# Layer 0 of a four-layer network: six instead of seven of eight half tiles convolved on TensorE, and other preferences in the schedule

## The chip, the cores and the metric

The kernel runs on one core of a Trainium2 chip. The metric is the device time of one execution in microseconds (us). Three runs of the kernel before gave 6812.61, 6817.96 and 6801.19 us, so the median is 6812.61 us. The engines are called by the profile's names: PE is TensorE (matmuls), PEld its weight loads, DVE VectorE, ACT ScalarE, POOL GpSimd, and SP the queue that issues most DMAs.

## The reference, cut to what matters

The input is a batch of 16 images with 96 channels of 56 x 56 pixels. Four layers follow each other. The change touches layer 0, a masked, channel-selected inverted bottleneck with a 3 x 3 depthwise convolution:

```python
logits = _conv1x1(x, w_mask) + b_mask[None, :, None, None]
mask = (logits >= 0).astype(x.dtype)
...
s = jax.nn.sigmoid(pooled @ w_sal.T + b_sal)
k = int(round(BUDGET * HID))
thr = lax.top_k(s, k)[0][:, -1:]
vector = (s >= thr).astype(x.dtype)
h = jax.nn.relu(_bn(_conv1x1(x, w_pw1), bn1_g, bn1_b, bn1_m, bn1_v)) * mask_dilate
h = h * vector[:, :, None, None]
h = jax.nn.relu(_bn(_dwconv3x3(h, w_dw), bnd_g, bnd_b, bnd_m, bnd_v)) * mask
h = h * vector[:, :, None, None]
h = _bn(_conv1x1(h, w_pw2), bn2_g, bn2_b, bn2_m, bn2_v) * mask
return x + h
```

Of 576 hidden channels each image keeps the 288 with the largest saliency. Layer 1 is a state-space block with scans, layers 2 and 3 are Fourier mixing with a quantized MLP. They stay as they are.

## The kernel before, in words

The four layers run one after the other: `layer0`, `layer1` and `layers23` each fill the core, and an image goes from one to the next through DRAM. A second version of layer 0 (`layer0_all`) stands behind a condition for inputs with a tie among the selected channels; it isn't executed here.

**Tiles of layer 0.** The 288 kept channels of an image are gathered into two full groups of 128 (group 0 and group 1) and a rest of 32. An image is cut into two halves of 28 rows. A half tile is 128 channels by 28 x 56 = 1568 pixels. For each image and group there are two half tiles; the rests of two images and both their halves are packed into one further tile, the mixed one (`MIX`). A pair of images therefore has nine tiles, the eight half tiles and the mixed one, and there are eight pairs. Among them are 32 half tiles of group 0.

**The path of a half tile** (`worker`). POOL clears the border row of a padded buffer (L797). PE multiplies the image by the chosen rows of the first weight (L816, tile `p`), ACT applies the batch norm and the relu and writes the padded buffer `pad` (L820). Then the 3 x 3 depthwise convolution follows, in one of two ways:

- On VectorE: one multiplication for the first tap (L863) and eight fused multiply-adds for the others (L865), each over the whole tile, 128 x 1568. ACT then applies norm and relu in place (L868).
- On TensorE: for each of two halves of the tile, nine taps times four 64 x 64 quarters of products with a diagonal weight, 36 products into the PSUM tile `p_c` (L838), from which ACT takes norm and relu in three pieces (L855).

`on_pe` decides which way it is: only tiles of group 0 go to TensorE, and of these all first halves, the second halves of even images, and those of images with b % 4 == 3. These are 28 of 32, or seven of eight. Group 1 and the mixed tile go to VectorE. VectorE thus has 32 + 4 half tiles and 8 mixed tiles.

**The choice of channels** (`vectors`), once for each image, ahead of its tiles: the image is loaded (L691) into one of four buffers `x`; ACT sums it (L695); VectorE makes the mean (L697, L699); PE forms the saliencies (`p_s`, L705); VectorE and ACT compare and count (L713, L720, L725, L726, L735, L737), with PE between them (`p_n`, L729 and L731); PE gathers the selected weights (`p_w` L744, `p_r` L752 and L758); ACT and VectorE copy them out (L747, L763, L770, L771, L775).

**The end of a half image** (`ends`), in two pieces: six products add up the three tiles (L887, L890), ACT takes the batch norm (L896), two products form the mask (`p_m`, L902), VectorE applies it and adds the image (L904, L907), and SP writes the result (L909). After the last piece the image buffer is free, and the next load may start.

**What sets the order.** Each of these steps is announced as an `Op` with an engine and an estimated cost. `in_order` keeps for every engine the time up to which it is planned, and again and again picks the step with the smallest sum of its possible start and a lead from a table (by engine and generator: `('DVE', 'ends')` is VectorE's part in `ends`); a negative lead lets a step go ahead of others. The pick is then emitted. So the table and the costs fix the order in which every engine executes, at the time of building; on the chip each engine takes its queue in that order and waits by semaphores. Buffers are planned too: four PSUM pairs `ps`, four images `x`, four padded buffers `pad`, twelve results `h`, two `y` and one `out`.

Of the kernel before, what the change touches and what calls it, by code (L numbers as in the profile page):

```python
# [59 lines left out]
def packed(x):  # L60
# [96 lines left out]
    for m in (C, DIN):  # L157
# [58 lines left out]
 'layer0': {'buffers': {'ps': 4, 'x': 4, 'pad': 4, 'h': 12, 'y': 2, 'out': 1},  # L216
            'leads': {('PE', 'worker'): 0.9,
                      ('DVE', 'worker'): 1.1,
                      ('DVE', 'ends'): 0.8,
                      ('ACT', 'vectors'): 0.1,  # L220
                      ('PE', 'filled'): 0.5,
                      ('ACT', 'ends'): -1.2,
                      ('ACT', 'filled'): -0.7,
                      ('SP', 'ends'): -0.2,
                      ('PE', 'vectors'): -0.1}},
 'layers23': {'buffers': {'ps': 4,
                          'xn': 2,
                          'xt': 1,
# [389 lines left out]
def layer0(ctx, tc, src, dst, flags):  # L618
# [49 lines left out]
        return Op("ACT", over + n * each, **k)  # L668

    def on_pe(b, g, half):  # L670
        return g == 0 and (b % 2 == 0 or half == 0 or b % 4 == 3)

    MIX = 2
    tiles = []
# [108 lines left out]
    def worker():  # L783
        while tiles:
# [40 lines left out]
            yield [filled(*run) for run in RUNS]  # L825
            h = hs[tile_] = buf([P, HALF * S], "h")
            if half != MIX and on_pe(b, g, half):
                taps, turn = its[0]["taps"][g], its[0]["turned"][g]
                for c in range(0, 4, 2):
# [1174 lines left out]
```

## Time and profile before

| | |
|---|---|
| median of three runs | 6812.61 us |
| the profiled execution | 6803.33 us |
| its span | 6801.4 us |
| PE, PEld, DVE, ACT, POOL busy over the span | 87%, 59%, 78%, 68%, 25% |
| mean granted clock of PE | 0.918 |
| layer 0 ends at | 1072 us |
| a VectorE tap (L865), 288 on half tiles | 1845 ns |
| the PE convolution (L838), 4032 records | 344.8 us busy |

The profile is one execution. Rows of groups give the line, the engine, the operation, output and input with shapes, the count, busy time and the mean of one in ns, and behind the last bar the engine's idle time just before and what ended it. A TensorE product of 32-bit numbers leaves two matmul records, so the 28 tiles of 72 products leave 4032. The records of one engine overlap a little; from start to start is the pace. Rows of waits give the waiting instruction, the one waited for, the total in us, the number and the longest. Rows in order of time begin with the start and the duration in us.

### The profile page before, as it was taken

The page shows a single profiled execution, that of the slowest core. Times are in us where ns is not written, and L with a number is a line of the kernel's source. Part 1 is how long each engine was busy: PE and PEld are TensorE (multiplying, and loading weights), DVE is VectorE, ACT ScalarE, POOL GpSimd, SP SyncE. Part 2 cuts the span into 40 slices and gives each one's busy share as a digit, 9 for nine tenths or more (in the row PEclk, how much of TensorE's full clock was granted, in tenths as well). Part 3 has the DMA queues.
Part 4 walks back from the last instruction along what each step waited for, and adds up shares of the span by engine and source line. Part 5 has one row for each costly group of instructions (what it writes and reads, how often), then busy time and mean ns, then how long its engine had stood idle before and what let it go on. Part 6 is the DMA issues. An engine that isn't in the chain of part 4 may idle for free.

```text
span 6801.4 us, 113297 instructions
## 1 busy us (share of the span) xinstructions
PE 5940.8 (87%) x45643; PEld 4042.6 (59%) x45643; DVE 5310.6 (78%) x6829; ACT 4627.4 (68%) x5959; POOL 1712.4 (25%) x1137
## 2 busy tenths in 40 slices
PE   7999997788888888888888776798999999999985
PEld 4455443244544455555555444687888888888875
DVE  6988892688888888888887893676787887878774
ACT  5555553788888888888888772466666666666664
POOL 0000001244444444444443442111111111111110
PEclk9999997788989888988889877899999999999997
DMA  1111111554444444444544441555555555555552
GB/s 41 42 40 36 40 29 51 147 149 139 141 135 142 137 135 142 134 143 141 145 132 126 125 133 53 118 116 125 129 121 127 120 125 134 138 137 121 123 112 64
DMA packets 508375, 763.72 MB, mean 112 GB/s; under 512 B 206337, under 2 KB 339137, under 8 KB 504530
## 3 DMA queue, kind: packets, MB, share of 16 engines
q1 hardware_dynamic: 506818, 753.53, 42.6%
q8 instruction: 362, 5.93, 0.4%
q0 software_dynamic: 1024, 2.85, 0.1%
q14 instruction: 171, 1.40, 0.1%
HBM read 563.65 MB, written 192.59 MB: 111 GB/s over the span
## 4 chain that ended last, share of the span: by engine, by line
PE 40%; DVE 33%; ACT 13%; issue 6%; DMA 5%; POOL 3%; SPq 1%; DVEq 0%; ACTq 0%; POOLq 0%
DVE h L865 4%; DVE dt L1345 4%; PE p_g L1511 3%; PE p_c L1209 3%; PE p_c L838 3%; DVE drive L1353 3%; DVE a L1359 2%; PE p_f L1501 2%; PE p_v L1803 2%; PE p_u L1821 2%; PE p_d L1276 2%; PE p L1756 2%; DVE hc L1325 2%; ACT big L1230 2%; PE p L1857 2%
## 5 line engine op out<-in xcount | busy, mean ns | idle before, releaser
L1382 POOL TENSOR_TENSOR big<-big,hc 128x784 f32<-128x784 f32 x384 | 776.5, 2022 | 1240.8 <-DVE hc L1325 1199.2
L1698 POOL TENSOR_TENSOR r<-v,nhalf 112x12 f32<-112x12 f32 (+1 forms) x128 | 357.0, 2798 | 2149.4 <-DVE v L1696 1263.1
L1345 DVE TENSOR_TENSOR dt<-dt,big 128x784 f32<-128x784 f32 x384 | 517.8, 1348 | 195.0 <-ACT a L1292 193.6
L865 DVE SCALAR_TENSOR_TENSOR h<-pad,rows,h 128x1568 f32<-128x1568 f32 x288 | 526.5, 1845 | 4.4
L1283 ACT ACTIVATE dt<-p_d,l_dtb 128x784 f32<-128x784 f32 x384 | 350.2, 912 | 176.0 <-PE p_d L1276 150.0
L1501 PE MATMUL p_f<-zt,w_fc 96*128 96x448 f32 x672 | 374.9, 704 | 85.2 <-ACT zt L1494 68.6
L1756 PE MATMUL p<-k_f,z 112*128 112x112 f32 x3072 | 392.1, 289 | 61.6 <-DVE h L1728 28.2
L1276 PE MATMUL p_d<-proj,l_dt 32*128 32x392 f32 x1536 | 391.0, 592 | 61.0 <-ACT hid L1503 36.3
L1353 DVE TENSOR_TENSOR drive<-dt,bc 128x784 f32<-128x784 f32 x384 | 430.3, 1121 | 9.3
L1209 PE MATMUL p_c<-x,taps 64*64 64x392 f32 x4608 | 425.5, 500 | 11.7 <-ACT big L1230 9.0
L1756 PEld LDWEIGHTS p<-k_f,z 112*128 112x128 f32 x3072 | 381.7, 205 | 72.5 <-issue 33.5
L1511 PE MATMUL p_g<-l_fc,hid 128*112 128x96 f32 x2688 | 393.7, 290 | 0.9 <-ACT hid L1503 0.9
L1325 DVE TENSOR_TENSOR hc<-a,bc 128x784 f32<-128x784 f32 x384 | 379.6, 989 | 3.1 <-POOL big L1382 3.1
L1285 ACT ACTIVATE dt<-dt,one 128x784 f32<-128x784 f32 x384 | 363.8, 947 | 9.3
L1511 PEld LDWEIGHTS p_g<-l_fc,hid 128*112 128x112 f32 x2688 | 358.2, 207 | 18.3 <-issue 10.7
L1734 PE MATMUL p<-h,k_f 112*128 112x192 f32 x1792 | 338.1, 337 | 31.7 <-DVE h L1728 17.3
L1292 ACT ACTIVATE a<-dt,aneg 128x784 f32<-128x784 f32 x384 | 348.1, 938 | 4.9 <-DVE a L1359 3.0
L1361 DVE TENSOR_TENSOR_SCAN a<-a,drive 128x784 f32<-128x784 f32 x192 | 350.2, 1824 | 0.5
L1359 DVE TENSOR_TENSOR_SCAN a<-a,drive 128x784 f32<-128x784 f32 x192 | 350.2, 1824 | 0.0
L1725 PE MATMUL p_a<-first,xt 97*112 97x192 f32 x1792 | 325.5, 333 | 27.4 <-ACT xt L1719 18.7
L838 PE MATMUL p_c<-pad,taps 64*64 64x392 f32 x4032 | 344.8, 491 | 0.1
L1725 PEld LDWEIGHTS p_a<-first,xt 97*112 97x112 f32 x1792 | 292.0, 180 | 55.1 <-ACT xt L1719 20.2
(339 smaller groups left out, 14268.0 us busy)
## 6 DMA issues: line engine op xcount, KB each, us to landing
bc<-bc SPq DMA_DIRECT2D x256, 784.0 KB
bc<-bc SPq DMA_DIRECT2D x256, 392.0 KB
d<-y SPq DMA_DIRECT2D x448, 192.0 KB
z<-d SPq DMA_DIRECT2D x128, 672.0 KB
d<-uu SPq DMA_DIRECT2D x256, 169.8 KB
z<-d SPq DMA_DIRECT2D x192, 194.0 KB
xc<-x SPq DMA_DIRECT2D x96, 336.0 KB
x<-in_x SPq DMA_DIRECT2D x16, 1176.0 KB
```

The source lines that it names most:

```text
L838: nc.tensor.matmul(p[to : to + 64, t, :TC], taps[64 * s : 64 * s + 64, i], pad[64 * s : 64 * s + 64, r0 : r0 + 7, i % 3 : i % 3 + S], star ...
L865: nc.vector.scalar_tensor_tensor(out, view, taps9[:, i : i + 1], out, ALU.mult, ALU.add)
L1209: nc.tensor.matmul(p[to : to + 64, b, :TC], taps[64 * s : 64 * s + 64, j, k], pad[64 * s : 64 * s + 64, r0 : r0 + 7, k % 3 : k % 3 + S], s ...
L1276: nc.tensor.matmul(p[:, b, :TC], wdt[on, i], proj[on, h], start=True, stop=True)
L1325: nc.vector.tensor_tensor(hc, a, t[:, 1], ALU.mult)
L1345: nc.vector.tensor_tensor(as_own(dt), as_own(dt), own(u), ALU.mult)
L1353: nc.vector.tensor_tensor(b, dt, t[:, 0], ALU.mult)
L1382: nc.gpsimd.tensor_tensor(out, out, hc, ALU.add)
L1501: nc.tensor.matmul(p[:, 0, :T], w_fc1[:, P * j : P * j + P], zt, start=True, stop=True)
L1511: nc.tensor.matmul(p[:Q, q, :C], hid[:, j, own], fc2[:, j], start=j == 0, stop=False)
L1725: nc.tensor.matmul(p[:Q, j, :HW], xt[:, at + j], w["first"], start=True, stop=True)
L1756: nc.tensor.matmul(p[:, q, :Q], flat[:, P * (3 * q + k) : P * (3 * q + k) + P], f2, start=True, stop=True)
```

## The change

The second halves of images 3, 7, 11 and 15 no longer fall to TensorE in `on_pe`, so that six of eight half tiles of group 0 stay there and VectorE convolves the others. The table of leads for layer 0 is another: some entries have other values (VectorE and SP in `ends` and PE in `vectors` change sign), the one of ACT in `filled` is gone, and those of POOL in `worker` and PE in `ends` are new. The numbers of buffers stay.

```diff
             'leads': {('PE', 'worker'): 0.9,
                       ('DVE', 'worker'): 1.1,
-                      ('DVE', 'ends'): 0.8,
+                      ('DVE', 'ends'): -0.2,
                       ('ACT', 'vectors'): 0.1,
                       ('PE', 'filled'): 0.5,
                       ('ACT', 'ends'): -1.2,
-                      ('ACT', 'filled'): -0.7,
-                      ('SP', 'ends'): -0.2,
-                      ('PE', 'vectors'): -0.1}},
+                      ('SP', 'ends'): 0.4,
+                      ('POOL', 'worker'): -2.6,
+                      ('PE', 'vectors'): 0.4,
+                      ('PE', 'ends'): -0.1}},
...
     def on_pe(b, g, half):
-        return g == 0 and (b % 2 == 0 or half == 0 or b % 4 == 3)
+        return g == 0 and (b % 2 == 0 or half == 0)
```

The changed program is one line longer ahead of these functions, so its lines from L226 on have a number higher by one: L838 becomes L839.

## The prediction

> **What bounds the kernel now.** The change lies in layer 0 alone; behind it the two programs issue the same instructions in the same order on all five engines. So I read layer 0 first: where it ends, then who is busy in it, then who waits in it. The stretches (us, busy time of PE, PEld, DVE, ACT, POOL, granted clock, DMA share, GB/s) say:
>
> ```profile
> 0.00:54.00 54.00, 18.64 (x91) 12.22 (x95) 14.46 (x56) 15.59 (x24) 13.09 (x24) 1.00 0.46 110
> 54.00:1072.00 1018.00, 1001.58 (x6692) 507.94 (x6684) 884.56 (x975) 551.22 (x735) 16.62 (x76) 1.00 0.13 34
> 1040.00:1072.00 32.00, 27.59 (x133) 13.13 (x123) 10.10 (x12) 7.60 (x8) 0.00 (x0) 0.99 0.16 48
> 1072.00:6801.00 5729.00, 4920.59 (x38868) 3522.43 (x38868) 4411.61 (x5798) 4060.58 (x5201) 1682.66 (x1037) 0.90 0.49 126
> ```
>
> Layer 0 ends at 1072: the next layer's first VectorE instruction waits there for the last output DMA. From the first VectorE convolution (54) on, PE is busy 98% of the time at full clock, VectorE 87%. Next, the groups that the change touches, and the waits of PE (54 to 1072) and of VectorE (54 to 1040, where its last convolution ends):
>
> ```profile
> L865 DVE SCALAR_TENSOR_TENSOR h<-pad,rows,h 128x1568 f32<-128x1568 f32 x288 | 526.5, 1845 | 4.4
> L838 PE MATMUL p_c<-pad,taps 64*64 64x392 f32 x4032 | 344.8, 491 | 0.1
> L863 DVE TENSOR_SCALAR h<-pad,rows 128x1568 f32<-128x1568 f32 x36 | 37.0, 1029 | 16.3 <-ACT pad L820 16.2
> ...
> PE p_s L705 <- DVE wide L699: 5.0, 3, 2.5
> PE p_n L729 <- DVE chosen L726: 2.9, 4, 2.3
> ...
> DVE y L904 <- PE p_m L902: 29.2, 9, 5.9
> DVE rest L770 <- ACT rows L763: 23.1, 6, 6.1
> DVE h L863 <- ACT pad L820: 16.2, 6, 4.6
> ```
>
> PE's waits come to 13 us in all, VectorE's (seven rows) to 104. So PE sets the pace and VectorE waits for what PE feeds it. Last, one turn of the image buffers, in order of time:
>
> ```profile
> 581.21 1.48 PE L902 MATMUL p_m<-x,l_mask 96*96 96x392 f32 x4
> 584.51 1.03 DVE L904 SCALAR_TENSOR_TENSOR y<-p_m,nmask,y 96x784 f32<-96x784 f32 x1
> 585.57 0.97 DVE L907 TENSOR_TENSOR out<-y,x 96x784 f32<-96x784 f32 x1
> 586.98 0.37 SPq L691 DMA_DIRECT2D x<-in_x  x1
> 594.62 2.82 ACT L695 ACTIVATE x<-x 96x3136 f32<-96x3136 f32 x1 [3.18 <-DMA x<-in_x]
> 597.56 0.15 DVE L697 TENSOR_SCALAR mean<-mean 96x1 f32<-96x1 f32 x1 [0.76 <-ACT x L695]
> 598.18 1.21 PE L705 MATMUL p_s<-l_sal,wide 97*128 97x288 f32 x4 [2.54 <-DVE wide L699]
> ```
>
> Image b+4 is loaded into the buffer that image b leaves: from the end of the last mask product of one (582.7) to the first product of the other (598.2) take 15.5 us, and PE waited 2.5 of them.
>
> **The change, part by part.**
>
> *Removed from PE.* on_pe loses the second half of images 3, 7, 11 and 15: 4 of 28 half tiles. Each costs 344.8/28 = 12.3 us of PE, together 49.3. Their six ACT evictions each (L855, (75.4+37.8)/28 = 4.0 us) give way to one L868 of 1.7: ACT loses 9 us and is busy 54% anyway, so I count nothing.
>
> *Added to VectorE.* Four times one L863 and eight L865. Busy time of such a tile is (526.5+37.0)/36 = 15.65 us, so 62.6 in all. It needs cover: 104 us of waits.
>
> *The order.* The other preferences change what stands behind what. In the old order 116 of 352 taps follow a tap of the same convolution, in the new one 26 of 384; elsewhere two convolutions alternate. The trace prices this: four taps in a row from 1022.89 to the next instruction at 1030.32, 1.86 each; alternating ones at 93.22, 94.99 and 96.75, 1.77 each. Ninety fewer pairs at 0.09 give 8 us back. So VectorE gets 54 us net. Output DMAs and image loads keep their number and sizes; the SP queue gains no entry in layer 0. The POOL queue keeps its pad memsets in number (80 and 0.2 us each), only in another order of pads.
>
> *PE alone.* Its last large product ended at 1067.2; less 49.3 gives 1018. From there to the layer's end is 4.9 as before (VectorE mask and add, then the last DMA): 1023.
>
> *VectorE alone.* From its first tap at 54: 48 tiles at 8 x 1.77 + 1.04 = 15.2 (730), 60 of the 64 output units at 1.03 + 0.97 = 2.0 (120; four stand behind the last tap), 15 selections of 6.1 (92: five L713, five L737, the small copies and L775), and the 9 us that it waits before 85, where the programs are still alike. The last tap ends at 1005. Behind it come L868 and a signal (1.9), then the products of the last image's half that still need it (fifteen in the order from the second on, 0.66 each: 9.9), then 4.9: 1022.
>
> Both queues alone thus reach about 1022, 50 below 1072. That is the limit of the gain. What is lost by their waiting for each other:
>
> (a) *The end.* In the new order the second mask product of image 12's second half has 92.7 us of PE work behind it (each product at its pitch in the trace: 0.66 us for 392 columns, 0.75 and 0.47 for the fills of 448 and 280, 6.1 for half a p_c tile), so PE reaches it at 1018 - 92.7 = 925. VectorE's L904 for it has 95 us of VectorE work behind it up to the last tap. So this tap can't end before 1020, and the layer not before 1020 + 16.7 = 1037. Loss 14. Late here is the last image: PE stands idle some 12 us before its last ten us of products.
>
> (b) *Image turns.* For images 4 to 14, even ones, the new order leaves 14.2 us of PE work between the two ends of the chain of the fourth block; it took 15.5 there. That is 1.3 for each of six images, 8 us; the old order had shorter distances twice (13.0 and 13.7 us), worth about 4. VectorE waits in the same turns, ahead of taps queued behind L697, but these are covered as PE is late by as much. Ends: 0 to 12; I take 4.
>
> (c) *The cold clock.* The row of 1040 to 1072 grants 0.99 to the last products, with no long gap ahead of them; by it (a)'s last 9.9 us cost 9.9. Against that speaks the Trainium skill, "TensorE: Matmul & The Clock Gate", section "What's actually happening": an array idle for one window of some 3.4 us is gated to half its clock, and comes back after some 3.4 us of activity. The change makes just such a gap. The trace agrees in kind: after PE's 10.3 us of idling at the layer's end the clock granted from 1075 to 1100 is 0.50. Half clock for 3.4 us adds 1.7, for all ten 9.9; I take 2, since the products are dense.
>
> (d) *The first 250 us.* VectorE is behind there, and products that reuse a PSUM buffer stand up to 6 us ahead of the L904 that frees it, as they already did. I take 2, ends 0 to 8.
>
> Sum: -50 + 14 + 4 + 2 + 2 = **-28 us**, the layer ends at 1044. Against the profiled execution (6803.33 us; span 6801.4, 1.9 around it) this gives 6775. The median of the runs shown is 6812.61, 9 above that execution; the forecast for the median is 6812.6 - 28 = **6784**.
>
> One reading has to be defended. The Trainium skill, "Perfetto Trace Analysis", section "Identifying the Most-Contended Engine", calls matmul busy time a bad measure and wants weight-load time instead. By that PE is loaded to 508/1018 = 50%, VectorE at 87% is the most contended, and 54 us more on it are a loss of up to 54. I hold with the waits: a busy row could hide slack, but an engine with slack would wait, and PE waits for others 13 us in 1018. A half tile's 36 products always take about 6.1 us, so they have no room to give.
>
> **The rivals.** *Clean gain*: image turns and end cost little more than (a) at its smallest, since VectorE's 54 us fit into 104 us of waits; about -43, 6770. Against it: the three ends above are in the order itself. *Half of it*: stalls chain, because both queues are full and only four pads and four PSUM pairs lie between them; each pair of images loses 2 to 3 us more, 8 x 2.5 = 20: -8, 6805. For it: old VectorE waits reach 6 us each. *VectorE becomes the bound, slower*: the place is L904 and L770, whose releasers (PE's mask product, ACT's copy of the rows) are fed late by VectorE itself. Its 104 us of waits would have to stay while its work grows: the last tap would end at 996 + 104 = 1100 and the layer at 1117, +45, 6857; taking half of the added work as lost, +20, 6833. It decides from the point where VectorE still waits over 59 us between first and last tap (1072 - 16.7 - 996). Against it: these waits are PE's pace, and PE is shortened. *That the change doesn't do what it says* can be excluded: the new program has 24 half tiles in L838's successor and 384 taps.
>
> **How the numbers follow.** Likeliest (-18 to -40) 0.64; clean (-40 to -50) 0.10; half (-18 to 0) 0.16; slower 0.10. A measurement of this kernel tells about 0.3% (20 us) from no change. Faster takes all of clean and 0.58 of the likeliest: 0.68. Same takes the remaining 0.06 and the half case: 0.22. Slower by over 20 us: 0.10, all of the third rival. The range leaves out that rival and the very best: 6765 to 6805; the likeliest alone is 6773 to 6795.
>
> **What would show it.** Right: L839 x3456 with about 296 us, L866 x320 with rows and x64 with the mixed tile, mostly 1.77 apart, layer 0's end (VectorE's wait for the last DMA) near 1044, VectorE over 95% busy from 54 to 1020, its waits there under 40 us, PE's waits up from 13 to about 30, one of them near the end of some 12 us. Everything after layer 0 unchanged in length. Wrong: VectorE's waits at 60 us or more, PE waits for L904 or L699 spread over all pairs, a clock under 0.95 inside layer 0, or a later layer that is longer.

## The result: 33 us faster, layer 0 ends 36 us earlier

The changed kernel takes 6776.68 us in the median of six runs (6767.66 to 6784.39), the one before 6809.85 in six runs on the same chip. The ratio is 0.995, with a 95% interval of 0.9937 to 0.9963: 33 us faster, where 28 were forecast (6784 against 6812.61); it lies inside the forecast's range of 6765 to 6805.

The stretches of the profile after (us, busy time of PE, PEld, DVE, ACT, POOL, granted clock, DMA share, GB/s):

```profile
54.00:1035.60 981.60, 957.98 (x6116) 486.02 (x6108) 935.31 (x1011) 541.25 (x716) 9.84 (x76) 0.99 0.13 35
1003.00:1035.60 32.60, 16.99 (x43) 7.41 (x43) 21.07 (x19) 7.17 (x6) 0.00 (x0) 0.76 0.16 47
1035.60:6777.00 5741.40, 4944.64 (x38868) 3535.66 (x38868) 4411.36 (x5798) 4063.01 (x5201) 1682.69 (x1037) 0.90 0.48 126
```

Layer 0 ends at 1035.6 instead of 1072.0. VectorE is busy 95% of it instead of 87%, PE still 98%. The last row is a warning on single profiles: with the same instructions in the same order, everything behind layer 0 took 5741.4 us here and 5729.4 before, so that the two spans differ by only 24.4. In the other profiles below this part takes between 5727 and 5747 us. I take that as noise, and use the layer's own end as the measure of the experiments. Each kernel has one profile, so how much the layer's end itself varies was not measured. Where a kernel ran four times or more, its median moved against before by the same as its layer's end to within 5 us; so a shift of 1 to 3 us of the end is not told from none.

The groups that answer to those shown of before, then PE's waits (54 to the layer's end) and VectorE's (54 to its last tap at 1016.2):

```profile
L866 DVE SCALAR_TENSOR_TENSOR h<-pad,rows,h 128x1568 f32<-128x1568 f32 x320 | 578.6, 1843 | 1.4
L839 PE MATMUL p_c<-pad,taps 64*64 64x392 f32 x3456 | 295.5, 491 | 1.0 <-DVE y L905 0.6
L864 DVE TENSOR_SCALAR h<-pad,rows 128x1568 f32<-128x1568 f32 x40 | 41.1, 1028 | 7.5 <-ACT pad L821 7.5
...
PE p L888 <- ACT h L869: 8.3, 1, 8.3
PE p_m L903 <- ACT y L897: 3.6, 1, 3.6
PE p_n L730 <- DVE chosen L727: 2.3, 1, 2.3
PE p_s L706 <- ACT y L897: 1.8, 1, 1.8
...
DVE y L905 <- PE p_m L903: 9.3, 13, 1.0
DVE h L864 <- ACT pad L821: 7.5, 2, 4.6
DVE mean L698 <- ACT x L696: 6.1, 8, 1.1
```

VectorE's waits went from 104 to 31 us in its seven rows; PE's from 13 to 20 in its eight, of which the first two, 11.9, lie at the very end. That end is this, on PE in order of time:

```profile
1001.51 0.82 PE L891 MATMUL p<-h,rest 128*96 128x392 f32 x2
1005.90 2.63 PE L903 MATMUL p_m<-x,l_mask 96*96 96x392 f32 x4 [3.57 <-ACT y L897]
1008.32 1.49 PE L888 MATMUL p<-h,rows 128*96 128x392 f32 x2
1018.09 1.62 PE L888 MATMUL p<-h,rows 128*96 128x392 f32 x2 [8.29 <-ACT h L869]
1019.51 1.51 PE L891 MATMUL p<-h,rest 128*96 128x392 f32 x2
1020.82 2.72 PE L888 MATMUL p<-h,rows 128*96 128x392 f32 x4
1023.37 0.82 PE L891 MATMUL p<-h,rest 128*96 128x392 f32 x2
```

PE waits for the last taps twice, and comes back slowly: two L888 records at 1008 last 1.49 and four at 1020 last 2.72, where four take 1.48 elsewhere. The clock granted in this stretch is 0.76, by the second row of the stretches. And one turn of an image buffer:

```profile
556.92 1.48 PE L903 MATMUL p_m<-x,l_mask 96*96 96x392 f32 x4
558.51 1.03 DVE L905 SCALAR_TENSOR_TENSOR y<-p_m,nmask,y 96x784 f32<-96x784 f32 x1 [0.23 <-ACT pad L821]
559.57 0.97 DVE L908 TENSOR_TENSOR out<-y,x 96x784 f32<-96x784 f32 x1
560.69 0.32 SPq L692 DMA_DIRECT2D x<-in_x  x1
567.95 2.82 ACT L696 ACTIVATE x<-x 96x3136 f32<-96x3136 f32 x1 [4.36 <-DMA x<-in_x]
570.89 0.15 DVE L698 TENSOR_SCALAR mean<-mean 96x1 f32<-96x1 f32 x1 [0.58 <-ACT x L696]
571.08 0.29 DVE L700 TENSOR_SCALAR wide<-ones,mean 97x128 f32<-97x128 f32 x1
572.63 1.14 PE L706 MATMUL p_s<-l_sal,wide 97*128 97x288 f32 x4
```

From the end of the mask product (558.4) to the first product of the next image (572.6) there are 14.2 us, all of it PE work; PE waits for nothing here, since the last step that it needs, L700, is done 13.0 us after the mask product. VectorE took the mask at once (0.1 us after the product; before it took 1.8), and the load was issued 0.15 us after the addition (before 0.44).

### The profile page after: what moved, and what is told of

Its sections match the earlier page's. It is cut to its first block, busy times and chain, and to the rows that moved or that the text cites. A ratio compares the mean times of both kernels' runs of the same rounds, so it can differ in the third digit from the quotient of the medians.

```text
span 6777.0 us, 112172 instructions
## 1 busy us (share of the span) xinstructions
PE 5921.0 (87%) x45067; PEld 4033.7 (60%) x45067; DVE 5361.1 (79%) x6865; ACT 4619.7 (68%) x5939; POOL 1705.6 (25%) x1137
## 4 chain that ended last, share of the span: by engine, by line
PE 38%; DVE 34%; ACT 13%; issue 6%; DMA 5%; POOL 3%; SPq 1%; ACTq 0%; DVEq 0%; POOLq 0%
DVE h L866 4%; DVE dt L1346 4%; PE p_g L1512 3%; PE p_c L1210 3%; DVE drive L1354 3%; PE p_f L1502 3%; PE p_v L1804 2%; PE p_u L1822 2%; DVE a L1360 2%; PE p_d L1277 2%; PE p_c L839 2%; DVE hc L1326 2%; PE p L1757 2%; ACT big L1231 2%; PE p L1858 2%
## 5 line engine op out<-in xcount | busy, mean ns | idle before, releaser
L866 DVE SCALAR_TENSOR_TENSOR h<-pad,rows,h 128x1568 f32<-128x1568 f32 x320 | 578.6, 1843 | 1.4
L1210 PE MATMUL p_c<-x,taps 64*64 64x392 f32 x4608 | 428.1, 503 | 11.9 <-ACT big L1231 9.2
L1726 PE MATMUL p_a<-first,xt 97*112 97x192 f32 x1792 | 325.0, 332 | 27.8 <-ACT xt L1720 18.9
L1735 PEld LDWEIGHTS p<-h,k_f 112*128 112x128 f32 x1792 | 294.0, 194 | 47.4 <-issue 21.8
```

What stands on the lines that cost most here:

```text
L866: nc.vector.scalar_tensor_tensor(out, view, taps9[:, i : i + 1], out, ALU.mult, ALU.add)
L1210: nc.tensor.matmul(p[to : to + 64, b, :TC], taps[64 * s : 64 * s + 64, j, k], pad[64 * s : 64 * s + 64, r0 : r0 + 7, k % 3 : k % 3 + S], s ...
L1726: nc.tensor.matmul(p[:Q, j, :HW], xt[:, at + j], w["first"], start=True, stop=True)
L1735: nc.tensor.matmul(p[:, j, :HW], f1[:, m0 + at + j], h[:, j], start=True, stop=True)
```

## The experiments

Eleven kernels ran. The table gathers where their layer 0 ends, where the last VectorE tap ends, and how long VectorE was idle from 54 to there (length of the stretch less its busy time).

| kernel | half tiles on PE | layer 0 ends | last tap ends | VectorE idle | median time (before beside it) |
|---|---|---|---|---|---|
| before | 28 | 1072.0 | 1039.8 | 111 | 6809.85 |
| changed | 24 | 1035.6 | 1016.2 | 35 | 6776.68 (6809.85) |
| tiles_only | 24 | 1086.9 | 1055.2 | 73 | 6824.42 (6807.65) |
| leads_only | 28 | 1066.8 | 1035.4 | 108 | 6803.94 (6807.65) |
| tiles_dve_ends | 24 | 1054.7 | 1035.0 | 53 | 6790.47 (6808.73) |
| tiles_two | 24 | 1055.9 | 1036.8 | 52 | 6788.70 (6810.23), one run |
| after_late_ends | 24 | 1053.3 | 1034.1 | 53 | 6796.58 (6808.73), one run |
| after_pe_vectors | 24 | 1045.0 | 1026.7 | 41 | 6780.50 (6810.23), one run |
| no_dve_taps | 24 | 1034.3 | 1015.6 | 75 | 6773.65 (6807.65), one run |
| no_pe_taps | 24 | 1036.2 | 1017.4 | 36 | 6765.53 (6807.65), one run |
| five_of_eight | 20 | 1118.0 | 1099.8 | 54 | 6853.37 (6808.73), one run |
| five_pool | 20 | 1167.0 | 1144.7 | 90 | 6899.21 (6808.73) |
| last_on_pe | 25 | 1032.7 | 1002.0 | 39 | 6766.89 (6810.23) |

**The two parts of the change, one at a time.** Only the tiles, with the leads of before:

```diff
     def on_pe(b, g, half):
-        return g == 0 and (b % 2 == 0 or half == 0 or b % 4 == 3)
+        return g == 0 and (b % 2 == 0 or half == 0)
```

> Only the four half tiles move to VectorE; the table of leads stays that of before. Theory (PE's load sets the pace): most of the 36 us is here, layer 0 ends between 1034 and 1050, time -22 to -38 against before. Rival (the order made by the leads does it): layer 0 ends at 1060 or later, time within 10 us of before.

And only the leads, with on_pe as before:

```diff
-                      ('DVE', 'ends'): 0.8,
+                      ('DVE', 'ends'): -0.2,
...
+                      ('POOL', 'worker'): -2.6,
+                      ('PE', 'vectors'): 0.4,
+                      ('PE', 'ends'): -0.1}},
```

> Only the leads change; PE keeps 28 of 32 half tiles. Theory: PE is as full as before, layer 0 ends at 1066 to 1080, time within 8 us of before. Rival (the leads do it): layer 0 ends near 1045, time -20 to -30.

The tiles alone make the kernel slower: ratio 1.002 (1.0013 to 1.0028), layer 0 15 us longer. That is the opposite of the theory; the rival had the layer's end (1060 or later), but not a loss of 17 us in the time. The leads alone are worth 5 us of layer 0, and the ratio is 0.9995 (0.9988 to 1.0002), as the theory had it. Together they bring 36. So neither part explains the gain: with 24 tiles on PE the order is worth 51 us, with 28 tiles 5. What the old order does with the moved tiles is seen in PE's waits of tiles_only:

```profile
PE p_w L744 <- DVE sel L737: 11.5, 9, 2.1
PE p_n L729 <- DVE chosen L726: 9.8, 4, 4.4
PE p L887 <- DVE y L904: 6.1, 1, 6.1
PE p_s L705 <- DVE wide L699: 5.9, 2, 5.6
PE p_m L902 <- DVE y L904: 5.8, 1, 5.8
PE p L816 <- DVE y L904: 5.4, 4, 2.5
```

Every one is a short step of VectorE that PE needs: the mask step of an image that ends, the comparisons of an image that begins. On VectorE itself, in order of time, one sees what is ahead of them:

```profile
1031.80 10.65 DVE L865 SCALAR_TENSOR_TENSOR h<-pad,rows,h 128x1568 f32<-128x1568 f32 x6
1042.38 1.02 DVE L904 SCALAR_TENSOR_TENSOR y<-p_m,nmask,y 96x784 f32<-96x784 f32 x1
1043.43 0.97 DVE L907 TENSOR_TENSOR out<-y,x 96x784 f32<-96x784 f32 x1
1044.33 10.90 DVE L865 SCALAR_TENSOR_TENSOR h<-pad,rows,h 128x1568 f32<-128x1568 f32 x6
1055.14 1.02 DVE L904 SCALAR_TENSOR_TENSOR y<-p_m,nmask,y 96x784 f32<-96x784 f32 x1
```

Six taps stand in front of each of the two mask steps L904, whose products PE had formed by 1032.1 and 1037.3; PE's waits of 6.1 and 5.8 us end with these two. Then VectorE in turn is fed late: it waits 31.8 us for filled pads (7.5 in the changed kernel). With the 28 tiles of before such steps were reached in time in either order; with 53 us more of work on VectorE they are not.

**Which lead.** The tiles, and of the leads only VectorE's in `ends`:

```diff
-                      ('DVE', 'ends'): 0.8,
+                      ('DVE', 'ends'): -0.2,
```

> The four half tiles move to VectorE, and of the leads only the one of VectorE in ends changes (0.8 to -0.2, the new kernel's value). With the old lead the mask steps of a finished image stood behind taps on VectorE, PE waited for them, and layer 0 ended at 1086.9. Theory (this lead is what makes the move pay): layer 0 ends at 1034 to 1045, time -25 to -36. Rival (several leads together, or those of PE and ACT): layer 0 ends at 1060 or later, time above -12.

The ratio is 0.9975 (0.9964 to 0.9987), layer 0 ends at 1054.7: 32 of the 51 us come back with this one entry, and PE's wait for L904 falls from 17 us to 9. It isn't all of it: the end lies between the theory's range and the rival's. The reverse, the changed kernel with this entry put back to 0.8:

> The changed kernel with only VectorE's lead in ends put back to 0.8. Theory: the waits of PE for mask steps and selections come back, layer 0 ends at 1065 to 1090 instead of 1035.6. Rival (the other leads suffice): at most 1045.

It ends at 1053.3, 18 later than the changed kernel; neither the theory nor the rival had that. With the other leads changed, the same entry is worth about half as much.

In tiles_dve_ends PE waited 16 us at L705, the first product of a loaded image, where the changed kernel waits 1.8. So I added PE's lead in `vectors`:

```diff
-                      ('PE', 'vectors'): -0.1}},
+                      ('PE', 'vectors'): 0.4}},
```

> As tiles_dve_ends (four tiles moved, VectorE's lead in ends at -0.2; layer 0 ended at 1054.7), and PE's lead in vectors at 0.4 as in the changed kernel. There PE waited 16 us at L705, the first product of a freshly loaded image. Theory (the rest of the difference to 1035.6 is this wait, since the lead puts other products ahead of L705): PE's wait at L705 falls under 5 us and layer 0 ends at 1036 to 1044. Rival (SP's, ACT's or PE's other leads): it ends above 1048.

The wait at L705 fell to 5.9 us, but layer 0 ended at 1055.9: the theory failed, the rival (above 1048) held. And the changed kernel with this lead put back:

> The changed kernel with PE's lead in vectors put back to -0.1. Theory: PE waits at L706 again and layer 0 ends 8 to 16 us later, at 1044 to 1052. Rival (this lead means nothing beside the others): 1033 to 1039.

It ended at 1045.0, 9 later, as the theory had it, though PE's waits at L706 were then only 4.1 us; a wait of 10.6 us stood elsewhere (L888 for L869, ACT's step behind the last taps). The number came out, the reason given for it not. So the entries don't add up: one by one put back they cost 18 and 9, while tiles_two, which lacks the three others (ACT in `filled`, SP and PE in `ends`), is 20 behind. In the order that the program plans, POOL's entry moves no instruction on PE, VectorE, ACT or SP; no run tried it alone. How the three others share the 20 was not tried either. What can be said is what the good order looks like: in the changed kernel every stretch of 120 us from 300 to 900 has PE busy 119.6 to 119.9 and VectorE 116.2 to 116.7, in tiles_two PE 115.6 to 118.4 and VectorE 111.1 to 115.4.

**Which engine is the bound after the change.** In the changed kernel's own order, VectorE leaves out taps:

```diff
-                    else:
+                    elif (b, g, half) not in ((3, 0, 1), (7, 0, 1), (11, 0, 1)):
                         nc.vector.scalar_tensor_tensor(out, view, taps9[:, i : i + 1], out, ALU.mult, ALU.add)
```

> The changed kernel in its own order, but VectorE leaves out eight of nine taps of the second halves of images 3, 7 and 11: 24 taps, 24 x 1.77 = 42 us of VectorE work gone. Theory (PE sets the pace and covers what VectorE took over; only the end, behind image 12, is VectorE's): layer 0 still ends at 1031 to 1037. Rival (VectorE has become the bound): it ends near 1036 - 42 = 994; both equally: 1010 to 1025.

Layer 0 ends at 1034.3: 42 us of VectorE work are worth 1.3 us, as the theory had it. The cover was real. Then PE leaves out taps:

```diff
-                    for i in range(9):
+                    many = 1 if half == 1 and b % 4 == 0 else 9
+                    for i in range(many):
...
-                                    start=i == 0, stop=i == 8,
+                                    start=i == 0, stop=i == many - 1,
```

> The changed kernel in its own order, but PE leaves out eight of nine taps of the second halves of images 0, 4, 8 and 12: 4 x 12.3 x 8/9 = 44 us of PE work gone. Theory: VectorE is right behind, so its own queue (last tap at 1005, layer 1022) takes over and layer 0 ends at 1018 to 1026, 10 to 18 us earlier instead of 44. Rival (VectorE far from full): it ends near 992. Rival (VectorE is the bound already): it stays at 1036.

It ends at 1036.2. So 44 us of PE work are worth nothing either, and my theory (10 to 18 earlier) was wrong, the last rival right. Taking either load away leaves the other queue as it is: the last tap ends at 1015.6 and 1017.4, against 1016.2. The change has brought the two queues to the same length, to within a few us. Both tests speak of the stretch ahead of the last mask product of image 12, which VectorE takes at 920.7 and 922.5 in them and at 921.5 in the changed kernel; the 95 us of VectorE work behind it they leave as they are.

**One step further.** Four more tiles to VectorE:

```diff
-        return g == 0 and (b % 2 == 0 or half == 0)
+        return g == 0 and (half == 0 or b % 4 == 0)
```

> The changed kernel with four more half tiles on VectorE (second halves of images 2, 6, 10 and 14): PE has 49 us less, VectorE 61 us more. Theory (after the change both queues are full, VectorE can take no more): its last tap goes from 1016 to about 1070, layer 0 ends at 1080 to 1095, 45 to 60 us after the changed kernel's and beyond the kernel before's. Rival (PE alone sets the pace): layer 0 ends near 990.

Layer 0 ends at 1118.0, 82 us later than with six of eight, and 46 later than before. The direction is the theory's, the size more than it had: besides 61 us of taps VectorE idles 54 instead of 35, since PE now waits for it (39 us for L869, ACT's step behind a tile's last tap, 24 for L700) and feeds it late.

Then the same with the additions given to GpSimd:

```diff
-                yield dve(2 * TC, take=("out",), give=("y", "x") if last and half else ("y",))
+                yield Op("POOL", 2.1, take=("out",), give=("y", "x") if last and half else ("y",))
                 out = buf([C, 2, TC], "out")
-                nc.vector.tensor_tensor(out, y, chunks(x[:, cols]), ALU.add)
+                nc.gpsimd.tensor_tensor(out, y, chunks(x[:, cols]), ALU.add)
```

> As five_of_eight, but the final addition of the image (L908, 64 times 0.97 us) is done by GpSimd instead of VectorE. This gives VectorE back 62 us, as much as the four tiles cost, and PE has 49 us less than in the changed kernel. Theory (both queues bind, so relieving both pays): layer 0 ends at 995 to 1020, time -50 to -75 against the kernel before. Rival (GpSimd's additions take too long or slow VectorE's taps, which run beside them): taps longer than 1.9 us, or layer 0 at 1030 or later.

The ratio is 1.0147 (1.0123 to 1.0171), layer 0 ends at 1167.0. The row of these additions (shortest, median and longest in ns), then those of the taps, of the first multiplications and of a comparison, with busy time and mean:

```profile
L908 POOL TENSOR_TENSOR out<-y,x x60: 1829/3468/18894, 135.3 to 1137.9; 96x784 f32<-96x784 f32 x60
...
L866 DVE SCALAR_TENSOR_TENSOR h<-pad,rows,h 128x1568 f32<-128x1568 f32 x352 | 654.6, 1894 | 2.0
L864 DVE TENSOR_SCALAR h<-pad,rows 128x1568 f32<-128x1568 f32 x44 | 59.9, 1365 | 7.8 <-ACT pad L821 7.7
L726 DVE TENSOR_SCALAR vec<-over 128x4 f32<-128x4 f32 (+1 forms) x32 | 11.2, 356 | 3.1 <-ACT more L721 3.0
```

The addition was planned with 2.1 us and can be done in 1.83, but took up to 18.9, 6.2 in the mean; the image is released only behind it, and VectorE's wait for the mean of the next image (L698) goes from 14 us in five_of_eight to 52. The taps grow by little (1894 instead of 1842 ns in five_of_eight), but other instructions of VectorE by much: L864 from 1027 ns to 1365 in the mean, L726 from some 150 to 356. Up to the last tap, VectorE's instructions other than mask steps and additions take 69 us more than in five_of_eight. That eats up the 62 us of additions taken off VectorE: up to there it is busy 1001 us, against 992 in five_of_eight. So the relief that the theory counted on did not come, and the rival was right: GpSimd's additions are slow, and they slow VectorE.

**The end.** Last, one tile back to PE, the one whose taps come last:

```diff
-        return g == 0 and (b % 2 == 0 or half == 0)
+        return g == 0 and (b % 2 == 0 or half == 0 or b == B - 1)
```

> The changed kernel, but the second half of image 15 stays on PE (25 of 32 half tiles). In the changed kernel PE idles 12 us ahead of its last ten us of products, for the last taps on VectorE. Theory (PE's own queue is the other limit, and this tile costs it 12 us): the idling goes, PE is busy with the tile instead, layer 0 ends at 1033 to 1040, the same time as the changed kernel within 5 us. Rival (the idling at the end was a pure loss): layer 0 ends at 1022 to 1028, 8 to 13 us faster than the changed kernel.

Layer 0 ends at 1032.7, 2.9 earlier, at the edge of the theory's range. PE works through to its end without either wait, and pays 12 us for the tile: the idling was not a pure loss. Its time is 6766.89 against 6810.23 beside it, ratio 0.9943 (0.9926 to 0.9959). It beats the kernel before; its lead over the changed kernel rests on the 2.9 us, since the intervals of the two ratios overlap.

## Why the prediction was right, step by step

*Removed from PE: right.* L839 has 3456 records and 295.5 us, 49.3 less.

*Added to VectorE: right.* Its busy time up to the last tap rose from 874.5 to 927.2, by 52.7; 54 were forecast, as the sum of 62.6 for the tiles and -8 for more alternation. The 8 were in part luck: the traces have 97 taps directly behind one of the same convolution before and 24 after, 1.89 us apart from start to start where others are 1.77. That is 73 pairs at 0.12 us, 9 us, where the forecast had ninety at 0.09.

*PE alone, 1018: right to 4 us.* Its large products ended at 1030.8. Less the 11.9 us of waits at the end, and the 1.8 and 2.8 us by which the products behind the two waits took longer, it is 1014. The 4 us are those of (b).

*VectorE alone, 1005 for the last tap: 11 too early.* It ended at 1016.2, and with 44 us less on PE at 1017.4. Its work was put too high (730 + 120 + 92 = 942 us, where VectorE was busy 927) and its idle time too low (9 us, where it was 35). The step counted no wait after 85; VectorE has some 18 us of them in pieces of about 1 us (mask steps, means), and they stay when PE has less to do. They follow from the order and from the way through other engines, not from PE's load; that last half is argued from no_pe_taps alone. It did no harm, because (a) was later.

*(a), the end: right.* This is the product of image 12 in the trace, and the mask step that takes it:

```profile
919.87 1.48 PE L903 MATMUL p_m<-x,l_mask 96*96 96x392 f32 x4
921.46 1.03 DVE L905 SCALAR_TENSOR_TENSOR y<-p_m,nmask,y 96x784 f32<-96x784 f32 x1 [0.23 <-ACT pad L821]
```

VectorE takes it 0.1 us after its end at 921.4, and the last tap ends at 1016.2, 94.8 us after L905 began; 95 were counted. PE idles 11.9 us in its two waits near there, with 12 forecast. What was off is the time at which PE gets there: 925 by (a) alone, 931 with the losses of (b) and (d), and 921.4 in the trace. That is why the last tap could end before the 1020 that were given as its earliest. But last_on_pe shows that the end is no free 12 us.

*(b), the image turns: wrong sign.* I took a loss of 4 us, because 14.2 us of PE work had to cover a chain that had taken 15.5. PE's waits at the first product of an image fell from 6.3 us (5.0 for L699, 1.3 for ACT) to 1.8 instead, a gain of 4.5. The chain isn't fixed: in the turn shown its last step before PE is done 13.0 us after the mask product, where it took 15.3 before; 1.7 of the difference is that VectorE takes the mask step at once. So 14.2 us of PE work cover it. This is the mis-sized term: it was off by 8.5 us, as much as the 8.4 by which the layer ended ahead of the forecast's 1044. The 2 us of (d) that did not come either are about made up by small excesses elsewhere, 0.8 of them in (c).

*(c), the cold clock: right.* From 1018.09 to 1030.8 the last products took 12.7 us where 9.9 would do: 2.8, with 2 taken. The rows of the end above show it in the trace: a wait of 8.3 us, then records of 1.5 and 2.7 where 0.8 and 1.5 are usual. The slow stretch lasts 5.3 us, from 1018.09 to 1023.37, where the 2 us rested on 3.4.

*(d), the first 250 us: nothing, where 2 us were taken.* PE's one wait there above 2 us is the same as before, 2.3 at L730 (before L729).

*Where the working was thinner than it looked.* It priced the order at 8 us, and called the 104 us of waits the cover for VectorE's new work. tiles_only has the same cover and the same 49 us less on PE, and loses 15 us. The forecast was saved by being counted along the new order itself, in (a) and (b); read as "49 us off PE, hidden on VectorE", it would have foretold a gain for tiles_only too, as I did in its expectation. That the step *The order* saw no more than 8 us in the order, where it is worth 51 with these tiles, did no harm for this reason alone. The third rival had the place (L904 fed and served late) and the sign; it describes tiles_only, not the changed kernel.

*The defended reading.* Weight-load time said that PE was half empty. no_dve_taps bears out the waits: with VectorE 42 us lighter the layer ends as before, so the queue that binds there is PE's, at 50% of weight-load time. no_pe_taps adds that VectorE's queue binds just as well.

## What to carry to other kernels

Work moved to an engine with idle time is hidden only if the engine's short steps, on which others wait, don't end up behind it: look at what stands in front of them in its queue before counting its idle time as cover. When both engines are near 95%, try order and split together; here each alone was worth little or less than nothing. Where taking work from either engine no longer moves the end, both queues are full: here 61 us of further taps then cost 82. Before giving work to a third engine, ask what the two share: here the relief of 62 us cost VectorE 69.

## What the runs showed of the hardware that I had not expected

An addition of two 96x784 tiles on GpSimd took 1.83 us at best, but 6.2 in the mean and 18.9 at worst while VectorE ran taps with two operands from SBUF back to back. It cost VectorE time too. One case of five_pool, in order of time:

```profile
668.88 3.60 DVE L866 SCALAR_TENSOR_TENSOR h<-pad,rows,h 128x1568 f32<-128x1568 f32 x2
669.09 5.11 POOL L908 TENSOR_TENSOR out<-y,x 96x784 f32<-96x784 f32 x1 [6.14 <-issue]
672.40 1.83 DVE L726 TENSOR_SCALAR vec<-over 128x4 f32<-128x4 f32 x1
```

The addition begins beside two taps and lasts until 674.20. The comparison L726 behind the taps, otherwise about 0.16 us for this form, takes 1.83 and ends at 674.23, together with the addition. That looks as if the addition made no way beside the taps and then held VectorE up for the 1.8 us that it needs; the trace doesn't show the wait itself. Up to 1150 us, 54 instructions of VectorE were longer by more than 0.15 us than the median of the same step in five_of_eight, by 78 us in all.

The Trainium skill, "GPSIMD Engine Reference", section "Key points", says that GpSimd shares its SBUF interfaces with VectorE, with contention from VectorE instructions that run in a 2-port perf mode or have two SBUF inputs. The trace agrees for the taps, which have two inputs, and shows that both engines pay. L726 and L864 read one tile; whether they run in such a mode, no run here shows. Whether the second operand of the taps is the cause was not tried apart.
